# Moving layernorm statistics, weight sums and gates within one attention kernel, and Silu in place of Sigmoid and a product

## The chip, the cores and the metric

The kernel runs on one core of a Trainium2 chip. TensorE (PE) multiplies matrices into PSUM banks; VectorE (DVE), ScalarE (ACT) and GpSimd (POOL) work elementwise; SyncE (SP) mostly issues DMAs, which POOL and ACT can issue too. Each engine works through a list of instructions in order and waits on semaphores. The metric is device time in microseconds (us), less is better.

## What is computed

The reference, for 4 batches of 512 rows and 1024 columns, all fp32:

```python
xn = layernorm(x)
# attention per batch, 16 heads of 64, rotary on q and k, causal
q, k, v = xn @ Wq, xn @ Wk, xn @ Wv
s = softmax(causal(rot(q) @ rot(k).T / 8)) @ v @ Wo
# gate, over all 2048 rows
r = softmax(xn @ gate_w.T)                     # 8 experts
h = (xn * (r @ in_scale)) @ sign(weight).T * (r @ out_scale) + bias
out = x + s * (h * sigmoid(h))
```

## The kernel before

**Projections and attention.** The work runs in 16 slots, four groups g of heads for each of four batches b; (3,2) below is b = 3, g = 2. In a slot, PE computes q, k and v of one group with products of matrix quarters (seven products instead of eight, `project_qk` L323 and `project_v` L403). Sums of quarters are made for that by DVE: `form_w` (L269) makes S1 to S4 of weights, `form_x` (L291) makes T1 to T4 of the transposed, normalised rows X. For the last batch T1 is written in place, over the quarter b12 of X. Rotary (L310) takes the finished c of q or k, makes four swapped copies on ScalarE (L316, L317), so eight for a pair of units, one DVE product (L318) and two POOL operations (L319, L320).

Between the projection's matmuls, the attention of the group before is woven in. A unit u is two heads. For a unit: `scores` (L505), `softmax` (L530: mask and maximum on DVE, Exp on ScalarE L548, scaling by 1/sum on POOL L558), `transpose_blocks` (L566: ten DVE transposes of 32x32 blocks L576, then 16 DMAs L586 that put the blocks in place) and `values` (L593: matmul pv L601, copy of v out of PSUM on ScalarE L610, store). The slot has 84 steps of projection matmuls, cut into 16 pieces; `attention_pieces` (L843) says at which piece which part is written, for two units and the rest of the group before:

```python
            2: lambda: v and transpose_blocks(v),
            3 if last else 4: values_and_scores(w, u0),
            4 if last else 6: lambda: softmax(u0, 2, 0),
            8 if last else 10: lambda: transpose_blocks(u0),
```

The order on PE is written out by hand: it is the program's order. On the other engines a scheduler places the instructions, except those held by `keep_in_program_order`. A ring of four PSUM banks serves the projections (pj), pv, part of the scores and the gate's products; the rest of the scores has two banks of its own. A PE product that needs the next bank waits until the last reader of that bank's earlier content is done.

**Layernorm of the next batch** runs in the slots g = 2 and g = 3 of the first three batches, one pair of tiles of 128 rows each: per tile two half statistics (L171), the aggregate and Sqrt (`deviation` L174, L179), then `normalize` (L182: reciprocal L186, product L187), later two PE transposes of half a tile (`transpose_x` L195, xtp L201) and a store of the normalised rows to xn_d. The slot loop (L887 to L947) starts tile t0 at the slot's start, and tile t0 + 1 at piece 7. Sqrt and Exp need different function tables on ScalarE; the compiler puts an ACT_TABLE_LOAD where the table changes.

**The turn.** After the last slot the attention of the last two units remains. Beside it the gate of pairs 0 and 1 is computed with plain matmuls (`ffn` L1000; a pair is two tiles of 128 rows), its results pass through `gate` (L1018: product on DVE L1021, bias on POOL L1022), and `sum_wo` (L988) makes four sums of quarters of Wo, in four chunks each, on DVE, the third on POOL (L996). The schedule stands at L1052 to L1087; `dense(gates, n, m)` issues n steps of the gate, and a chunk of a sum after each of the first m. `values(u0)` and `values(u1)` come last.

**Output projection.** For pairs q = 0 to 7, `project_out` (L1213) multiplies the attention rows (ap) by Wo in seven products (wo, L1235), with sums of ap by `form_a` (L1096), and adds x and the gate. The `silu` (L1026) of pairs 0 and 1 is written just before this loop; for q from 2 on it follows each gate. `sign_sum` (L1115) makes four sums of sign matrices that the gates from pair 2 on need. `ahead` (L1335 on) lists what is written between the products of `project_out`, one entry at each of its stops (its yields).

Of the kernel before, what the change touches and what calls it, by code (L numbers as in the profile page):

```python
# [9 lines left out]
F32 = mybir.dt.float32  # L10
F32R = mybir.dt.float32r
AF = mybir.ActivationFunctionType
# [11 lines left out]
P = 128  # L24
# [18 lines left out]
def attn_gated_ffn_kernel(  # L43
# [138 lines left out]
    def normalize(b, t):  # L182
        xt = xin[b, t]
        mv, std = MV[b, t]
        rstd = st.tile([P, 1], F32, tag="rstd", name=f"rstd_{b}_{t}")
        nc.vector.reciprocal(rstd, std)  # L186
        nc.vector.tensor_scalar(xt, xt, mv[:, 0:1], rstd, op0=ALU.subtract, op1=ALU.mult)  # L187

    def layernorm(b, t):
        half_statistics(b, t, 0)  # L190
        half_statistics(b, t, 1)
        deviation(b, t)
        normalize(b, t)

    def transpose_x(b, t, g):  # L195
        if b not in X:
# [94 lines left out]
    def form_x(b, n):  # L291
        b11, b12, b21, b22 = quarters_x(b)
        if n > 1:
            f = fp.tile([P, 4, TH], F32, tag=f"T{n}", name=f"T{n}_{b}")
        elif b < B - 1:

            f = sgp.tile([P, 4, TH], F32, tag="last", name=f"T1_{b}")
        else:

            f = b12  # L300
        TF[b, n] = f
        x0, x1 = {
            1: lambda: (b12, b11),
            2: lambda: (b22, TF[b, 1]),
            3: lambda: (b22, b12),
            4: lambda: (b21, TF[b, 2]),
        }[n]()
        nc.vector.tensor_tensor(f, x0, x1, op=ALU.subtract)
# [534 lines left out]
    def attention_pieces(k, late):  # L843

        units = [(*groups[k], i) for i in range(2)]
        w, v = late
        u0, u1 = units

        def values_and_scores(before, u):
            def both():  # L850
                if before:
                    values(before)
                scores(u)
                softmax(u, 1, 3)

            return both

        pieces = [[] for _ in range(16)]  # L860

        last = k == len(groups) - 2
        plan = {
            2: lambda: v and transpose_blocks(v),
            3 if last else 4: values_and_scores(w, u0),
            4 if last else 6: lambda: softmax(u0, 2, 0),
            8 if last else 10: lambda: transpose_blocks(u0),
            9 if last else 12: values_and_scores(v, u1),
            10 if last else 14: lambda: softmax(u1, 2, 0),
        }  # L870
        if last:
            plan[14] = lambda: transpose_blocks(u1, ordered=True)
        for n, piece in plan.items():
            pieces[n].append(piece)
        return pieces, units
# [11 lines left out]
    for k, (b, g) in enumerate(groups):  # L887
        pieces = [[] for _ in range(9)]
        if k > 0:
            pieces, late = attention_pieces(k - 1, late)  # L890

        def at(n, piece):
            pieces[n].append(piece)


        if g == 0:
            routing = [lambda n=n: router(b, n) for n in range(3)]
            if k == 0:
                at(0, routing[0])
                at(1, lambda: (load_scales(in_scale), load_scales(out_scale)))  # L900
                at(2, routing[1])
                at(4, routing[2])
                at(5, lambda: split_scales(isc))
            else:
                if b < B - 1:
                    at(5, routing[0])
                at(8, routing[1])
                at(15, routing[2])
        elif g == 1 and b + 1 < B:

            at(11, lambda: [load_x(b + 1, t) for t in range(2)])
            if b == 0:
                at(1, lambda: split_scales(osc))
        elif g > 1 and b + 1 < B:
            t0 = 2 * (g - 2)
            layernorm(b + 1, t0)
            at(7, lambda: layernorm(b + 1, t0 + 1))
            for n, t, h in ((8, t0, 0), (9, t0, 1), (13, t0 + 1, 0), (14, t0 + 1, 1)):
                at(n, lambda t=t, h=h: transpose_x(b + 1, t, h))
            if g == 2:  # L920
                at(11, lambda: load_x(b + 1, 2))
                at(15, lambda: load_x(b + 1, 3))
        if k in (5, 9, 12, 14):
            n = {5: 0, 9: 2, 12: 4, 14: 6}[k]
            at(0, lambda: (load_sign(n), load_sign(n + 1)))
            at(8, lambda: make_sign(n))
            at(15, lambda: make_sign(n + 1))
        if b == B - 1:

            if g < 2:  # L930
                load_xn(g)
            if g in (1, 2):
                at(1, lambda: in_scales(g - 1, score_banks))
            if g == 3:
                z_place[0] = [xip.tile([P, E], F32, tag="x", name=f"z0_{i}") for i in range(2)]
                at(1, lambda: out_scales(0, score_banks))
        if k == 11:

            at(15, lambda: router(b + 1, 0))
        interleave(pieces, fill, 3 * 7 * 4 if k else 3 * 7 * 4 - 8)  # L940
        if g == NGRP - 1:
            for _ in fill:
                pass
            if b + 1 < B:
                for n in (3, 1, 2, 4):
                    form_x(b + 1, n)
                fill = projections(b + 1)  # L947
    pctx.close()
# [39 lines left out]
    def sum_wo(n, c):  # L988
        out_, x0, x1 = {
            1: (t1, b12, b11),  # L990
            2: (t2, b22, t1),
            3: (t3, b22, b12),
            4: (t4, b21, t2),
        }[n]
        engine = nc.gpsimd if n == 3 else nc.vector
        difference = engine.tensor_tensor(out_[:, c, :], x0[:, c, :], x1[:, c, :], op=ALU.subtract)  # L996
        if n != 3:
            tc.keep_in_program_order(difference)

    def ffn(q, i, k):  # L1000

# [23 lines left out]

    def silu(q, i, k):  # L1026
        z = Z[q, i][:, k * HALF : (k + 1) * HALF]
        g = work.tile([P, HALF], F32, tag="g", name=f"g_{q}_{i}_{k}")
        nc.scalar.activation(g, z, AF.Sigmoid)
        nc.gpsimd.tensor_tensor(z, z, g, op=ALU.mult)  # L1030

    def gated(q):
        for i in range(2):
# [13 lines left out]

    u0, u1 = units = [(*groups[-1], i) for i in range(2)]
    w, v = late
    sums = iter([(n, c) for n in (1, 3, 2, 4) for c in range(4)])  # L1050

    def dense(gates, n, n_sums=0):  # L1052
        for i in range(n):
            next(gates)
            if i < n_sums:
                sum_wo(*next(sums))
# [7 lines left out]
    dense(gates, 8)  # L1064

    split(1, 0)
    transpose_blocks(u0, ordered=True)
    load_wo(1)
    values(v)
    scores(u1)  # L1070
# [7 lines left out]
    out_scales(1, score_banks)  # L1078
    dense(gates, 2)
    transpose_blocks(u1, (nc.sync, nc.scalar), ordered=True)  # L1080
    dense(gates, 10, 10)
    values(u0)
    dense(gates, 2, 2)
    values(u1)
    for _ in gates:
        pass
# [28 lines left out]
    def sign_sum(n):  # L1115

        if n == 3:
            TS[n] = [sg[4], sg[5]]
        else:
            t = (app if n == 4 else tsp).tile(  # L1120
                [P, 2, E], F32R, tag="ap" if n == 4 else f"T{n}", name=f"Tsg{n}"
            )
            TS[n] = [t[:, r, :] for r in range(2)]
        for r in range(2):
            x0, x1 = {
                1: lambda: (sg[4 + r], sg[r]),
                2: lambda: (sg[6 + r], TS[1][r]),
                3: lambda: (sg[6 + r], sg[4 + r]),
                4: lambda: (sg[2 + r], TS[2][r]),
            }[n]()  # L1130
            nc.vector.tensor_tensor(
                TS[n][r], x0.bitcast(F32), x1.bitcast(F32), op=ALU.subtract
            )

    PARTS = {}
# [185 lines left out]
            )  # L1321

    load_xn(2)

    for q in range(2):
        for i in range(2):
            for k in range(2):
                silu(q, i, k)
    for q in range(len(pairs)):
        if q < 2:  # L1330
            for n in range(1, 5):
                form_a(q, n)
        if q == 0:
            load_at(1)
        ahead, later = [], []  # L1335
        if q == 0:
            ahead = [lambda n=n: sign_sum(n) for n in (1, 2, 3)]
        elif q < len(pairs) - 1:
            ahead = [
                lambda: None,  # L1340
                lambda: (in_scales(q + 1), later.append(first_parts(q + 1))),
                lambda: out_scales(q + 1),
                lambda: later.pop()(),
            ]
        for _ in project_out(q):
            if ahead:
                ahead.pop(0)()
        if q != 1 and q + 1 < len(pairs):
            load_at(max(q + 1, 2))
        if q == 1:  # L1350
            sign_sum(4)
        if 1 <= q < len(pairs) - 1:
            gated_by_strassen(q + 1)
            if q + 2 < len(pairs):
                load_xn(q + 2)
# [58 lines left out]
```

## Time and profile before

| | us |
|---|---|
| median of 3 runs (lowest to highest) | 1114.5 (1114.41 to 1115.24) |
| profiled execution | 1114.49 |
| its span | 1112.6 |
| PE busy | 1086.9 |
| DVE, POOL, ACT busy | 896.9, 575.5, 469.9 |
| POOL multiplies of silu (L1030), 32 of them | 47.6 |
| ACT_TABLE_LOAD for Sqrt (L179) and Exp (L548), 12 each | 15.4 and 15.4 |
| first PE instruction, end of the last | 1.5, 1108.1 |

The slots end and the turn begins near 785 us; the loop over pairs begins near 824 us and takes the rest. The mean clock granted to PE is 0.998 of full speed.

How to read it: the first part of the page gives busy time, share of the span and number of instructions of each engine. A group of instructions is named by its line, engine, and what it writes and reads (`p<-sc,nmx` writes p from sc and nmx). A row of the waits says which engine and line waited, after the arrow for what, then the total in us, how often, and the longest. A row of a timeline gives the start, the time from the first start to the last end of the instructions in it, their number, and in brackets how long the engine was idle before and what ended that. Instructions that follow one another overlap by about 0.1 us. A stretch's granted clock comes from a table by windows.

### The profile page before, as it was taken

The page shows a single profiled execution, that of the slowest core. Times are in us where ns is not written, and L with a number is a line of the kernel's source. Part 1 is how long each engine was busy: PE and PEld are TensorE (multiplying, and loading weights), DVE is VectorE, ACT ScalarE, POOL GpSimd, SP SyncE. Part 2 cuts the span into 40 slices and gives each one's busy share as a digit, 9 for nine tenths or more (in the row PEclk, how much of TensorE's full clock was granted, in tenths as well). Part 3 has the DMA queues.
Part 4 walks back from the last instruction along what each step waited for, and adds up shares of the span by engine and source line. Part 5 has one row for each costly group of instructions (what it writes and reads, how often), then busy time and mean ns, then how long its engine had stood idle before and what let it go on. Part 6 is the DMA issues. An engine that isn't in the chain of part 4 may idle for free.

```text
span 1112.6 us, 15955 instructions
## 1 busy us (share of the span) xinstructions
PE 1086.9 (98%) x5176; PEld 788.0 (71%) x5176; DVE 896.9 (81%) x1736; ACT 469.9 (42%) x1080; POOL 575.5 (52%) x594
## 2 busy tenths in 40 slices
PE   9999999999989999998999999999979999999998
PEld 8887677787768778776877787777744545655664
DVE  7887989788897978889787987887797777667764
ACT  2553665454366545436653452664520222122220
POOL 0672555555255555525552662674585455444535
PEclk9999999999999999999999999999999999999999
DMA  9415556644655664465566544554683222431431
GB/s 322 144 60 149 174 148 159 194 136 120 178 168 155 169 177 135 120 180 168 159 169 195 171 149 141 151 131 127 165 252 114 81 91 103 156 118 47 142 114 57
DMA packets 86898, 163.88 MB, mean 147 GB/s; under 512 B 13472, under 2 KB 49056, under 8 KB 80800
## 3 DMA queue, kind: packets, MB, share of 16 engines
q1 hardware_dynamic: 80528, 152.91, 46.2%
q0 software_dynamic: 4576, 8.39, 2.2%
q10 hardware_dynamic: 1712, 1.57, 0.5%
q8 instruction: 41, 0.67, 0.3%
q14 instruction: 41, 0.34, 0.1%
HBM read 95.45 MB, written 25.43 MB: 109 GB/s over the span
## 4 chain that ended last, share of the span: by engine, by line
PE 74%; DVE 11%; POOL 4%; issue 3%; ACT 3%; DMA 2%; SPq 1%; POOLq 0%; DVEq 0%; ACTq 0%
PE pj L335 25%; PE wo L1235 16%; PE pj L422 13%; PE ff L1175 7%; PE sc L522 5%; PE pv L601 5%; POOL p L558 2%; DVE y L576 2%; DVE S L289 2%; DVE nmx L545 1%; SPq L586 1%; PE xtp L201 1%; DVE w L289 1%; DMA xn_d<-X 1%; ACT sw L317 1%
## 5 line engine op out<-in xcount | busy, mean ns | idle before, releaser
L558 POOL TENSOR_SCALAR p<-p,rs 128x256 f32<-128x256 f32 (+3 forms) x256 | 181.8, 726 | 189.0 <-DVE rs L556 144.3
L548 ACT ACTIVATE p<-sc,nmx 128x256 f32<-128x256 f32 (+3 forms) x256 | 132.8, 529 | 92.9 <-DVE nmx L545 72.6
L319 POOL TENSOR_TENSOR sw<-sw,sin_sb 128x512 f32<-128x512 f32 x64 | 89.6, 1400 | 94.4 <-ACT sw L317 93.0
L335 PE MATMUL pj<-X,w 128*128 128x256 f32 x576 | 134.4, 382 | 0.2 <-ACT X L207 0.2
L335 PE MATMUL pj<-T,S 128*128 128x256 f32 x512 | 118.2, 381 | 8.5 <-ACT v L610 7.2
L335 PEld LDWEIGHTS pj<-X,w 128*128 128x128 f32 x576 | 108.1, 190 | 18.6 <-issue 2.9
L576 DVE STREAM_TRANSPOSE y<-p 128x256 f32<-128x256 f32 x320 | 110.2, 408 | 12.7 <-POOL p L558 12.7
L316 ACT ACTIVATE sw<-c 32x512 f32<-32x512 f32 x128 | 80.3, 628 | 81.0 <-DVE c L349 79.3
L335 PEld LDWEIGHTS pj<-T,S 128*128 128x128 f32 x512 | 96.0, 190 | 23.6 <-ACT v L610 8.8
L335 PE MATMUL pj<-T,w 128*128 128x256 f32 x448 | 107.2, 382 | 0.0
L545 DVE TENSOR_REDUCE nmx<-sc 128x1 f32<-128x256 f32 (+3 forms) x160 | 104.9, 683 | 1.3
L320 POOL TENSOR_TENSOR rot<-rot,sw 128x512 f32<-128x512 f32 x64 | 94.1, 1470 | 5.0
L335 PEld LDWEIGHTS pj<-T,w 128*128 128x128 f32 x448 | 83.3, 190 | 15.2 <-issue 4.6
L422 PE MATMUL pj<-w,X 128*128 128x256 f32 x416 | 93.8, 380 | 0.0
L422 PEld LDWEIGHTS pj<-w,X 128*128 128x128 f32 x416 | 78.7, 190 | 11.0 <-issue 0.5
L542 DVE TENSOR_TENSOR sc<-sc,mask 128x256 f32<-128x256 f32 (+1 forms) x160 | 57.2, 371 | 30.8 <-PE sc L522 30.8
L317 ACT ACTIVATE sw<-c 32x512 f32<-32x512 f32 x128 | 80.4, 628 | 1.7
L522 PE MATMUL sc<-rot,rot 64*128 64x128 f32 (+3 forms) x512 | 80.3, 444 | 0.4 <-DVE v L448 0.3
L422 PE MATMUL pj<-w,T 128*128 128x256 f32 x352 | 80.2, 381 | 0.0
L610 ACT COPY v<-pv 128x512 f32<-128x512 f32 x32 | 18.6, 581 | 145.6 <-PE pv L601 132.7
L385 POOL TENSOR_TENSOR part<-part,part 128x256 f32<-128x256 f32 x32 | 25.9, 809 | 102.1 <-ACT part L384 81.8
L601 PE MATMUL pv<-p,v 128*64 128x256 f32 (+3 forms) x512 | 76.0, 439 | 2.7 <-DVE xp L996 2.7
(177 smaller groups left out, 2042.9 us busy)
## 6 DMA issues: line engine op xcount, KB each, us to landing
p<-y SPq DMA_DIRECT2D x504, 80.0 KB, 2.1
w<-in_wqk SPq DMA_DIRECT2D x31, 1024.0 KB, 5.3
w<-in_wv SPq DMA_DIRECT2D x16, 1024.0 KB, 5.2
x<-in_x SPq DMA_DIRECT2D x16, 512.0 KB, 3.5
at_d<-v SPq DMA_DIRECT2D x32, 256.0 KB, 2.7
xp<-xn_d SPq DMA_DIRECT2D x16, 512.0 KB, 4.5
ap<-at_d SPq DMA_DIRECT2D x16, 512.0 KB, 5.0
xr<-in_x SPq DMA_DIRECT2D x32, 256.0 KB, 3.0
```

The source lines that it names most:

```text
L317: nc.scalar.activation(sw[r + 32 : r + 64, :], c[r : r + 32, :], AF.Copy, scale=sc)
L319: nc.gpsimd.tensor_tensor(sw, sw, sin_sb, op=ALU.mult)
L320: nc.gpsimd.tensor_tensor(rot, rot, sw, op=ALU.add)
L335: nc.tensor.matmul(ps, lhsT=wq[:, k, :], rhs=xq[:, k, :], start=(k == 0), stop=(k == 3))
L422: nc.tensor.matmul(ps[:, j, :], lhsT=xq[:, k, j * P : (j + 1) * P], rhs=wq[:, k, :], start=(k == 0), stop=(k == 3),)
L522: nc.tensor.matmul(head(i, h), lhsT=Q[u][r : r + D, i * P : (i + 1) * P], rhs=K[u][r : r + D, : (i + 1) * P], start=True, stop=True,)
L545: nc.vector.tensor_reduce(nmx[:, hs], v, AX.X, ALU.max, negate=True)
L548: nc.scalar.activation(pt[:, h, :], ps[h], AF.Exp, bias=nmx[:, h : h + 1], accum_out=ssum[:, h : h + 1],)
L558: nc.gpsimd.tensor_scalar(pt[:, h, :], pt[:, h, :], rs[:, h : h + 1], 1.0, op0=ALU.mult, op1=ALU.mult,)
L576: nc.vector.transpose(out[:, :, :, o : o + 32], src.rearrange("p h (b c) -> p h b c", b=4))
L601: nc.tensor.matmul(by_block[r : r + D, :, 32 * j :], lhsT=V[u][:, j, r : r + D], rhs=PT[u][:, :, o : o + 32 * (TPB - j)], start=(j == 0), ...
L1235: nc.tensor.matmul(ps, lhsT=lhs[:, k, :], rhs=rhs[:, k, :], start=(first and k == 0), stop=(k == 3), skip_group_check=not first,)
```

## The change

1. In the six layernorm slots the statistics of both tiles are written at the slot's start, followed by the normalize of t0; that of t0 + 1 comes at piece 3. The PE transposes of t0 move from pieces 8 and 9 to 7 and 8.
2. `transpose_blocks(u0)` is written at piece 9 instead of 10, except in the last slot.
3. For the last batch, T2 is T3 + b11 instead of b22 - T1 (the same value), and the order is 3, 2, 4, 1.
4. `silu` is one Silu on ScalarE, in place, without the POOL product. For pairs 0 and 1 it is written inside the first `project_out`, at its second and fourth stop.
5. All weight sums are on VectorE and in program order: 1 and 2 before the loop over pairs, 3 after the third sum of `form_a(0, ...)`, 4 at the second stop of the first `project_out`.
6. The sign sums are held in program order and are spread over the first two pairs.
7. The DMAs of `transpose_blocks(u0)` in the turn are issued by SP and POOL in turn instead of SP alone.

```diff
--- before.py
+++ after.py
@@ -186,11 +186,10 @@
         nc.vector.reciprocal(rstd, std)
         nc.vector.tensor_scalar(xt, xt, mv[:, 0:1], rstd, op0=ALU.subtract, op1=ALU.mult)
 
-    def layernorm(b, t):
+    def layernorm_scales(b, t):
         half_statistics(b, t, 0)
         half_statistics(b, t, 1)
         deviation(b, t)
-        normalize(b, t)
 
     def transpose_x(b, t, g):
         if b not in X:
@@ -299,6 +298,10 @@
 
             f = b12
         TF[b, n] = f
+        if b == B - 1 and n == 2:
+
+            nc.vector.tensor_tensor(f, TF[b, 3], b11, op=ALU.add)
+            return
         x0, x1 = {
             1: lambda: (b12, b11),
             2: lambda: (b22, TF[b, 1]),
@@ -864,7 +867,7 @@
             2: lambda: v and transpose_blocks(v),
             3 if last else 4: values_and_scores(w, u0),
             4 if last else 6: lambda: softmax(u0, 2, 0),
-            8 if last else 10: lambda: transpose_blocks(u0),
+            8 if last else 9: lambda: transpose_blocks(u0),
             9 if last else 12: values_and_scores(v, u1),
             10 if last else 14: lambda: softmax(u1, 2, 0),
         }
@@ -913,9 +916,12 @@
                 at(1, lambda: split_scales(osc))
         elif g > 1 and b + 1 < B:
             t0 = 2 * (g - 2)
-            layernorm(b + 1, t0)
-            at(7, lambda: layernorm(b + 1, t0 + 1))
-            for n, t, h in ((8, t0, 0), (9, t0, 1), (13, t0 + 1, 0), (14, t0 + 1, 1)):
+
+            layernorm_scales(b + 1, t0)
+            layernorm_scales(b + 1, t0 + 1)
+            normalize(b + 1, t0)
+            at(3, lambda: normalize(b + 1, t0 + 1))
+            for n, t, h in ((7, t0, 0), (8, t0, 1), (13, t0 + 1, 0), (14, t0 + 1, 1)):
                 at(n, lambda t=t, h=h: transpose_x(b + 1, t, h))
             if g == 2:
                 at(11, lambda: load_x(b + 1, 2))
@@ -942,7 +948,7 @@
             for _ in fill:
                 pass
             if b + 1 < B:
-                for n in (3, 1, 2, 4):
+                for n in (3, 1, 2, 4) if b + 1 < B - 1 else (3, 2, 4, 1):
                     form_x(b + 1, n)
                 fill = projections(b + 1)
     pctx.close()
@@ -992,10 +998,9 @@
             3: (t3, b22, b12),
             4: (t4, b21, t2),
         }[n]
-        engine = nc.gpsimd if n == 3 else nc.vector
-        difference = engine.tensor_tensor(out_[:, c, :], x0[:, c, :], x1[:, c, :], op=ALU.subtract)
-        if n != 3:
-            tc.keep_in_program_order(difference)
+        tc.keep_in_program_order(
+            nc.vector.tensor_tensor(out_[:, c, :], x0[:, c, :], x1[:, c, :], op=ALU.subtract)
+        )
 
     def ffn(q, i, k):
 
@@ -1025,9 +1030,7 @@
 
     def silu(q, i, k):
         z = Z[q, i][:, k * HALF : (k + 1) * HALF]
-        g = work.tile([P, HALF], F32, tag="g", name=f"g_{q}_{i}_{k}")
-        nc.scalar.activation(g, z, AF.Sigmoid)
-        nc.gpsimd.tensor_tensor(z, z, g, op=ALU.mult)
+        nc.scalar.activation(z, z, AF.Silu)
 
     def gated(q):
         for i in range(2):
@@ -1047,7 +1050,7 @@
 
     u0, u1 = units = [(*groups[-1], i) for i in range(2)]
     w, v = late
-    sums = iter([(n, c) for n in (1, 3, 2, 4) for c in range(4)])
+    sums = iter([(n, c) for n in (1, 2, 3, 4) for c in range(4)])
 
     def dense(gates, n, n_sums=0):
         for i in range(n):
@@ -1064,7 +1067,7 @@
     dense(gates, 8)
 
     split(1, 0)
-    transpose_blocks(u0, ordered=True)
+    transpose_blocks(u0, (nc.sync, nc.gpsimd), ordered=True)
     load_wo(1)
     values(v)
     scores(u1)
@@ -1078,9 +1081,9 @@
     out_scales(1, score_banks)
     dense(gates, 2)
     transpose_blocks(u1, (nc.sync, nc.scalar), ordered=True)
-    dense(gates, 10, 10)
+    dense(gates, 10, 4)
     values(u0)
-    dense(gates, 2, 2)
+    dense(gates, 2)
     values(u1)
     for _ in gates:
         pass
@@ -1128,8 +1131,10 @@
                 3: lambda: (sg[6 + r], sg[4 + r]),
                 4: lambda: (sg[2 + r], TS[2][r]),
             }[n]()
-            nc.vector.tensor_tensor(
-                TS[n][r], x0.bitcast(F32), x1.bitcast(F32), op=ALU.subtract
+            tc.keep_in_program_order(
+                nc.vector.tensor_tensor(
+                    TS[n][r], x0.bitcast(F32), x1.bitcast(F32), op=ALU.subtract
+                )
             )
 
     PARTS = {}
@@ -1321,26 +1326,34 @@
             )
 
     load_xn(2)
-
-    for q in range(2):
-        for i in range(2):
-            for k in range(2):
-                silu(q, i, k)
+    def silu_pair(q):
+
+        for i, k in ((0, 0), (1, 1), (1, 0), (0, 1)):
+            silu(q, i, k)
+
     for q in range(len(pairs)):
         if q < 2:
             for n in range(1, 5):
                 form_a(q, n)
+                if q == 0 and n == 3:
+                    for c in range(4):
+                        sum_wo(3, c)
         if q == 0:
             load_at(1)
         ahead, later = [], []
         if q == 0:
-            ahead = [lambda n=n: sign_sum(n) for n in (1, 2, 3)]
+            ahead = [
+                lambda: None,
+                lambda: (silu_pair(0), [sum_wo(4, c) for c in range(4)]),
+                lambda: sign_sum(1),
+                lambda: silu_pair(1),
+            ]
         elif q < len(pairs) - 1:
             ahead = [
-                lambda: None,
+                lambda: q == 1 and sign_sum(2),
                 lambda: (in_scales(q + 1), later.append(first_parts(q + 1))),
                 lambda: out_scales(q + 1),
-                lambda: later.pop()(),
+                lambda: (later.pop()(), q == 1 and sign_sum(3)),
             ]
         for _ in project_out(q):
             if ahead:
```

## The prediction, on record before the change was run

> **What bounds the kernel now.** I read the page first. TensorE (PE) is busy for 1086.9 of 1112.6 us, and PE carries 74% of the chain that ended last. So a microsecond on another engine counts only where PE waits for it. The waits of PE alone say where:
>
> ```profile
> PE 1086.9 (98%) x5176; PEld 788.0 (71%) x5176; DVE 896.9 (81%) x1736; ACT 469.9 (42%) x1080; POOL 575.5 (52%) x594
> PE pj L335 <- ACT v L610: 7.2, 4, 1.9
> PE xtp L201 <- ACT p L548: 4.2, 3, 1.4
> PE wo L1235 <- ACT g L1029: 3.0, 1, 3.0
> PE pv L601 <- DVE xp L996: 2.7, 1, 2.7
> PE pj L335 <- DVE T L308: 1.3, 1, 1.3
> PE os L780 <- ACT p L548: 0.3, 1, 0.3
> ```
>
> In each row (us in total, times, longest) the name after the arrow is the work that ended last. Outside the start and the end, PE has some 19 us to lose, and these rows are nearly all of it. From 845 us on, where pair after pair runs at one beat, the PE timeline has no gap. So the trace's windows that matter are six places: three slots with layernorm (139, 334, 528 us, alike), 592 us, 628 us, and the turn from attention to projection (784 to 836 us).
>
> The second view is the timeline of ScalarE (ACT) in the first layernorm slot:
>
> ```profile
> 132.05 0.63 ACT L316 ACTIVATE sw<-c 32x512 f32<-32x512 f32 x1 [6.65 <-DVE c L349]
> 135.16 0.56 ACT L610 COPY v<-pv 128x512 f32<-128x512 f32 x1
> 135.74 0.63 ACT L317 ACTIVATE sw<-c 32x512 f32<-32x512 f32 x1
> ...
> 137.66 1.28 ACT L548 ACT_TABLE_LOAD   x1
> 138.96 0.47 ACT L548 ACTIVATE p<-sc,nmx 128x256 f32<-128x256 f32 x1
> ```
>
> Eight rotary copies (L316/317) wait for DVE's c. The copy of v, which frees the bank of pv for PE's next product, stands behind five of them, and PE waits 1.79 us for it (135.77). The Exp stands behind all eight and a table load; PE waits 1.38 us for it (139.58). Both waits start at the late c.
>
> The third view is PE in the turn:
>
> ```profile
> 822.09 2.37 PE L601 MATMUL pv<-p,v 128*64 128x512 f32 x16 [2.68 <-DVE xp L996]
> 824.39 3.70 PE L1235 MATMUL wo<-wo,ap 128*128 128x512 f32 x8
> 831.12 5.37 PE L1235 MATMUL wo<-xp,S 128*128 128x512 f32 x8 [3.03 <-ACT g L1029]
> ```
>
> Of the two eight-record products the second took 5.2 us (831.12 to 836.32) instead of 3.43. The granted clock was 0.56 from 831.1 to 834.0 and 0.82 to 836.4. The two waits cost 2.68 + 3.03, and the clock 1.77 more.
>
> **The change, part by part.** Where a price depends on order, I use the order of instructions that each engine's program has after the change; it is static and holds no times.
>
> *Layernorm in three slots.* Statistics of both tiles move to the start, so the second half of the slot loses two statistics (1.27 us a pair), the aggregate and a normalize (1.03), 2.65 us of DVE with the rest. Each Sqrt between Exps costs two table loads of 1.28; six slots go from four to two, 12 fewer. At the slot's start the added DVE work lies beside PE work: its S3 waits for a weight that lands at 120.66, and PE's first wait comes 15 us later. If that cover were gone, 2.65 us would show. The c of the second half should come about 2 us earlier (130.0 instead of 132.05). But in ScalarE's new order v is behind all eight copies, not five. Eight copies (0.64 each) and v end at 130.0 + 5.1 + 0.6 = 135.7, as before (135.72). So the first stall stays; the second, with its table load gone, should go: 3 × −1.4 = **−4.2**. Bounds: −4.7, and −1 if c gains only a little. Slots g = 3 have no PE wait: 0, unless the one-piece-earlier transposes (x at pieces 7 and 8, p at 9) delay something.
>
> *Transposes of p at piece 9, and v behind more copies, in slots without layernorm.* In slots (1,0) and (2,0) v moves from behind five copies to behind eight. The row near 230 us: copies start at 230.39, v ends at 234.06, PE takes the bank at 234.47 with no wait. With c 0.45 earlier, v ends near 235.65: a new stall of about 1.3, twice: **+2.6** (1.6 to 4.6). In slot (3,0) DVE's transposes now wait for POOL's p (L558, 614.4 against 612.95), c is 0.9 later and v one copy (0.64) further back: **+1.5** (0.7 to 2.1) on the 1.86 already there. In (3,2) DVE waits likewise (712.2), c moves to 717.6, v ends at 723.4 where PE wants it at 721.1: **+2.3** (1.5 to 2.8).
>
> *Last batch's T2.* It is made as T3 + b11 instead of b22 − T1, and is second in line. T1 is written in place, so it waits until the store of xn_d has landed:
>
> ```profile
> 589.96 1.23 DVE L308 TENSOR_TENSOR X<-X 128x1024 f32<-128x1024 f32 x1 [6.91 <-DMA xn_d<-X]
> 592.48 1.23 DVE L308 TENSOR_TENSOR T<-X,T 128x1024 f32<-128x1024 f32 x1
> ```
>
> T2 and T4 no longer stand behind it; DVE had been idle for 6.91 us. The stall of 1.26 at 592.50 goes: **−1.3** (0 if T1 is next to be late).
>
> *Silu in one function.* Sixteen Sigmoid halves and 32 POOL multiplies (47.6 us in all, 1.46 to 1.53 each) become Silu in place. In the beat after 845 us no PE wait hangs on them: 0. There the hiding work is PE's own; removing POOL work can't speed it. Whether a Silu takes longer than a Sigmoid (0.63) the trace doesn't show; up to 1.3 would still fit, ScalarE being busy for 53 of 230 us there.
>
> *The turn.* Taken away: POOL's sum (5.43 us) and eight multiplies (15.5), moved in part to DVE (4 × 0.68). With POOL active, DVE's sums took 1.0 to 1.75 and one 4.74 instead of 0.68, so DVE gains more than it gets. The Trainium skill's "GPSIMD Engine Reference" (4.1 Engine selection) advises VectorE for tile add and multiply and calls GpSimd about twice as slow with two inputs; the rows say 1.27–1.38 against 0.68. Added: the Silus of pairs 0 and 1. They are written later, but the scheduler has put two of them early, between the Exps of the last two softmaxes, each with a load there and a load back. What a load costs decides here:
>
> ```profile
> 825.10 1.28 ACT L1029 ACT_TABLE_LOAD   x1
> 826.40 1.15 ACT L1029 ACTIVATE g<-z 128x512 f32<-128x512 f32 x2
> ```
>
> The next function starts 1.30 after the load. The skill's "ScalarE: Activation LUTs" (What ACT_TABLE_LOAD costs) adds a drain of 1.38, 2.66 us per switch. By the page, two switches would put 5.3 + 0.6 us before the Exp; by the row 2.6 + 0.6, less its idle 1.08 before: 2.1 later (789.7 for 787.57). I take the row. The u0 transposes come 1 us later; the Exps of u1, whose load inherits their wait, end 1.45 later (os stall 0.35 to 1.8: **+1.5**). POOL now issues eight of the p loads too (about 0.55 each), ahead of u1's scaling, which had slack of 6.45, and is done by 808.2 as before. DVE's transposes of u1 end 1.1 later and PE's pv (822.09) is 1.0 later, **+1.0**. By then DVE has sums 1 and 2 and then S2 without POOL beside it: ready near 824.5, against 831 now. So the wait of 3.03 goes, pv's delay is left, and PE's product starts at about 828.85 instead of 831.12. As the two idles no longer follow one another, I expect the clock to stay up: −1.77. The skill's "TensorE: Matmul & The Clock Gate" (Part 1) puts the drop at an idle window of 3.4 us. Neither idle reached that, yet the clock fell after 2.68 and 3.03 within 12 us, so the row allows that pv's wait alone (some 3.7) drops it again: by the page the slow clock stays, by the nearest rows (single waits up to 1.9, clock 1.00) it goes. Net of the turn, 828.85 − 831.12 − 1.77 = **−4.0**, which contains the two plus terms; range −5 to +1.5.
>
> **Sum.** −4.2 + 2.6 + 1.5 + 2.3 − 1.3 − 4.0 = −3.1. The profiled execution took 1114.49 for a span of 1112.6, and the median is 1114.5, so both sums start at the same point: **1111.4 us**, −0.28%.
>
> **Rivals.**
> 1. *The copies of v don't hurt.* If c gains more than 2 us, or the bank's wait is covered by another bank of the ring, the +6.4 vanish: 1105. For it: four banks. Against: today's v waits hit this very place.
> 2. *Slower: the copy of v behind all eight copies.* One mechanism in up to eight slots: three more copies are 1.9 us. If c does not come earlier in the layernorm slots (because DVE's queue refills with the moved transposes), their first stall grows by 1.9 − 0.7 each instead of shrinking: +3.6 in place of −4.2, hence −3.1 + 7.8 = +4.7 with the turn as forecast: 1119; with half of it, 1116. It decides as soon as c gains less than about 1 us. Against: 2.65 us of DVE work does leave that stretch.
> 3. *No change.* The stalls move to another row, as in the first stall above, and the turn's Silus eat its gain: within 2 us of 1114.5. The change doesn't do what it says in one point: gates "later" are early in ScalarE's program.
>
> **Chances.** A measurement of this kernel tells about 0.2% (2.2 us) from no change. My forecast (1109 to 1113) 0.40, rival 1 (below 1109) 0.14, no change 0.22, rival 2 (above 1116.7) 0.24. The forecast's upper edge lies within the 0.2%. So faster 0.49, same 0.21, slower 0.30. The range, 1107 to 1117, takes in the bounds of the turn and half of each rival.
>
> **What would show it.** Right: no wait of xtp on Exp in the slots at 139, 334, 528 us; none at 592; PE waits on v (L613 after the change) in (1,0), (2,0), (3,0), (3,2) of 1.2 to 3.5 us; 19 table loads; the wo product after 828 us at clock 1.00. Wrong: v waits missing at 234 us (rival 1) or three times above 2.5 us in layernorm slots (rival 2); a second slow-clock stretch in the turn; or waits of PE in the beat after 845 us, which would mean that Silu is dearer than I took it.

## The result, and the profile after

| | before | after |
|---|---|---|
| median of 5 runs, us (lowest to highest) | 1115.24 (1114.41 to 1117.05) | 1110.42 (1109.2 to 1111.51) |
| ratio, 95% interval | | 0.9952 (0.9939 to 0.9965) |
| profiled execution / its span | 1114.49 / 1112.6 | 1110.42 / 1108.7 |
| end of the last PE instruction | 1108.07 | 1103.03 |
| POOL busy | 575.5 | 518.9 |

The change saves 4.8 us by the medians; the forecast was 1111.4, a saving of 3.1. The waits of PE after the change (total, times, longest):

```profile
PE pj L338 <- ACT v L613: 8.5, 7, 2.3
PE os L783 <- ACT p L551: 2.0, 1, 2.0
...
PE pj L338 <- ACT p L551: 1.5, 2, 1.1
PE pj L425 <- ACT p L551: 0.5, 1, 0.5
PE pv L604 <- issue: 0.4, 1, 0.4
```

The rows of xtp on Exp (4.2), of wo on the gate (3.0), of pv (2.7) and of T (1.3) are gone. The row of v has grown from four waits to seven, os (the product with the output scales, r @ out_scale) waits 2.0 instead of 0.3, and Exp appears as a cause at new places. So the kernel took out some 11 us of waits and let in about 5 us.

ScalarE in the first layernorm slot:

```profile
129.78 0.63 ACT L319 ACTIVATE sw<-c 32x512 f32<-32x512 f32 x1 [4.02 <-DVE c L352]
...
134.92 0.59 ACT L613 COPY v<-pv 128x512 f32<-128x512 f32 x1
135.53 0.47 ACT L551 ACTIVATE p<-sc,nmx 128x256 f32<-128x256 f32 x1
```

By the traces' own times the copies start 2.3 us sooner (132.05 before). PE itself runs 0.60 later here in this execution, so against PE they start 2.9 sooner. No table load stands before Exp, and v is behind all eight copies. PE's wait on v is 1.20 us here (1.79 before).

PE in the turn:

```profile
822.58 2.38 PE L604 MATMUL pv<-p,v 128*64 128x512 f32 x16 [0.36 <-issue]
824.88 3.70 PE L1240 MATMUL wo<-wo,ap 128*128 128x512 f32 x8
828.42 3.60 PE L1240 MATMUL wo<-xp,S 128*128 128x512 f32 x8
831.85 3.60 PE L1240 MATMUL wo<-wo,ap 128*128 128x512 f32 x8
```

No bracket stands at 828.42: the wait of 3.03 is gone, and the product takes its 3.43 us, at full clock. But the granted clock now falls earlier, behind the wait on v in slot (3,0) and behind the wait of os. A row gives the window, its length, PE busy, granted clock, DMA share and GB/s:

```profile
624.00:626.00 2.00, 2.00 (x7) 0.60 0.51 115
626.00:628.00 2.00, 2.00 (x7) 0.55 0.46 104
...
804.00:806.00 2.00, 1.35 (x5) 0.83 0.88 313
806.00:808.00 2.00, 2.00 (x6) 0.50 0.99 293
808.00:810.00 2.00, 2.00 (x9) 0.82 0.96 356
```

For a sum that misses nothing I subtract the start of the same PE instruction in two traces, at the borders of the stages. What a stage adds to that difference is what it gained or lost, in waits and in clock:

| stage (us against before) | forecast | after | what the waits say |
|---|---|---|---|
| layernorm slots, three pairs | -4.2 | -3.67 | v 1.20, 1.38, 1.39 for 3 x 1.79; xtp 3 x 1.38 gone; Exp 0.37, 1.12, 0.48, 0.14, 0.14 new |
| slots (1,0) and (2,0) | +2.6 | +0.92 | v 0.18 each |
| last batch's T2 (592 us) | -1.3 | -1.73 | 1.26 gone |
| slot (3,0) | +1.5 | +1.33 | v 2.34 for 1.86; the clock fell |
| slot (3,2) | +2.3 | +2.08 | v 1.81 |
| turn, up to 845 us | -4.0 | -4.01 | os 2.01 for 0.35, pv 0.36 for 2.68, 3.03 gone; the clock fell behind os, not behind 3.03 |
| pairs from 845 us on | 0 | -0.57 | no row shows it, see below |
| sum | -3.1 | -5.65 | |

The stages begin 0.6 us later in this execution, and from the last matmul to the end of the span it takes 1.1 us longer (5.66 against 4.56), which leaves 3.9 us of span.

A wait costs more than its row says, by about 0.27 us: the wait of 0.18 in slot (1,0) cost 0.44, that of 1.81 in (3,2) cost 2.08, and one of 1.77 with the layernorm order alone cost 2.04. A matmul there takes 0.38 us and the next starts 0.21 us after it, and a bracket does not count the overlap that is lost. At the start of slot (2,2) it is 0.7 us, for which no row gives a reason.

The table compares one execution of each kernel; of 55 others of the kernel before, timed beside the experiments, the eight with a mean granted clock of 1.000 took 1111.4 to 1112.6 us, and the twenty at 0.992 or less took 1114.2 to 1117.3.

### The profile page after: what moved, and what is told of

It is laid out like the page before. It is cut to its first block, busy times and chain, and to the rows that moved or that the text cites. A ratio compares the mean times of both kernels' runs of the same rounds, so it can differ in the third digit from the quotient of the medians.

```text
span 1108.7 us, 15895 instructions
## 1 busy us (share of the span) xinstructions
PE 1087.4 (98%) x5176; PEld 790.2 (71%) x5176; DVE 870.4 (79%) x1740; ACT 461.3 (42%) x1072; POOL 518.9 (47%) x566
## 5 line engine op out<-in xcount | busy, mean ns | idle before, releaser
L338 PE MATMUL pj<-T,S 128*128 128x256 f32 x512 | 120.5, 385 | 8.5 <-ACT v L613 8.5
L322 POOL TENSOR_TENSOR sw<-sw,sin_sb 128x512 f32<-128x512 f32 x64 | 85.1, 1330 | 81.1 <-ACT sw L320 75.4
L323 POOL TENSOR_TENSOR rot<-rot,sw 128x512 f32<-128x512 f32 x64 | 90.8, 1419 | 5.0
```

Source lines behind the costliest of these rows:

```text
L322: nc.gpsimd.tensor_tensor(sw, sw, sin_sb, op=ALU.mult)
L323: nc.gpsimd.tensor_tensor(rot, rot, sw, op=ALU.add)
L338: nc.tensor.matmul(ps, lhsT=wq[:, k, :], rhs=xq[:, k, :], start=(k == 0), stop=(k == 3))
```

## The experiments

Each kernel ran on a chip beside the kernel before; the ratios are to that.

**Layernorm order alone.** Edit of the kernel before: part 1 of the change.

> The kernel before with the layernorm order alone (part 1 of the change); all else as before. My theory, from the two traces: in the three slots g = 2 the wait of xtp on Exp (1.38 each) goes and the wait on v falls from 1.79 to 1.2 to 1.4, while DVE's added work at the slot's start makes the first Exp of the slot late for PE by 0 to 1.1 us: about -3 us against before, no new wait of more than 0.5 in slots g = 3. Rival (the fewer table loads alone matter): -4.2 and no wait on Exp at the slots' starts. Rival (nothing; the whole gain is elsewhere): within 1 us of before, the stalls move to the row of v.

Measured: 1105.18, ratio 0.992 (0.9898 to 0.9943), some 9 us for the expected 3. In the slots g = 2 no wait on v and none of xtp is left. (The profiled execution, at 1108.65, was the slowest of four.) ScalarE there:

```profile
129.01 0.63 ACT L315 ACTIVATE sw<-c 32x512 f32<-32x512 f32 x1 [4.49 <-DVE c L348]
...
132.12 0.56 ACT L609 COPY v<-pv 128x512 f32<-128x512 f32 x1
132.70 0.63 ACT L316 ACTIVATE sw<-c 32x512 f32<-32x512 f32 x1
```

v is still behind five copies, ends at 132.68, and PE wants its bank at 133.94. The layernorm slots gain 6.95 us (3.67 with the whole change), and the wait at 592 us shrinks from 1.26 to 0.45. At the starts of slots new waits on Exp came: 0.31 and 1.17 in slots g = 2, as expected, and 1.77 and twice 0.25 in slots g = 3, where 0.5 at most was expected. PE now reaches these places sooner, and DVE's maxima, for which Exp waits, do not come sooner by as much. Both rivals fall, and so does my own picture that the layernorm order puts v behind eight copies. The edit also moves two transposes one piece earlier; the two were not taken apart.

**Silu alone.** Edit of the kernel before:

```diff
-        nc.scalar.activation(g, z, AF.Sigmoid)
-        nc.gpsimd.tensor_tensor(z, z, g, op=ALU.mult)
+        nc.scalar.activation(z, z, AF.Silu)
```

> The kernel before with Silu in place of Sigmoid and the POOL product, nothing moved. Theory that the turn's gain comes from taking POOL's products away from beside DVE's sums: the wait of 3.03 before the second wo product falls below 1.2 us, no slow clock behind it, and the whole is 2 to 4 us below before, although two Silus come early between the Exps and the wait of os grows to 2.0. Rival, that the gain comes from moving the weight sums behind the first products: the wait of 3.03 stays over 2.5, and with the early Silus the time is at or up to 1.5 us above before.

Measured: 1117.13, ratio 1.0026 (1.0017 to 1.0036): slower. Its waits of PE:

```profile
PE pj L335 <- ACT v L610: 7.2, 4, 1.9
PE os L780 <- ACT p L548: 4.2, 1, 4.2
PE pv L601 <- DVE z_t L996: 2.4, 1, 2.4
```

Half of the theory holds: without POOL's products the wait of 3.03 is gone. But the early Silus make os wait 4.17 us, the clock falls to 0.50 for some 6 us, and the turn costs 1.40 more; the pairs after 845 us give 0.92 of that back. The clock also fell behind the waits on v at 137, 331, 526 and 629 us, where in the trace of before the same waits left it at 1.00. In slot (3,0) that cost 1.47; in the three slots g = 2 only 0.1 each, because PE, being slower, no longer met the wait of xtp (1.38).

**Silus held.** Edit of the changed kernel:

```diff
-        nc.scalar.activation(z, z, AF.Silu)
+        gated = nc.scalar.activation(z, z, AF.Silu)
+        if q < 2:
+            tc.keep_in_program_order(gated)
```

> The changed kernel with the eight Silus of pairs 0 and 1 held in program order on ScalarE, so behind the last Exps; four table loads fewer. Theory that the early Silus cost what the wait of os and the slow clock behind it show (2.01 us and about 1.4 more): os waits 0.4 us, no slow clock at 806 us, and the time is 1 to 2.5 us below the changed kernel. Rival: PE only waits later, for the blocks of p of the last unit (pv near 822 us), and the time is within 0.5 us of the changed kernel.

Measured: 1110.2, ratio 0.9966 (0.995 to 0.9981); no gain over the change, so the rival holds. os waits 0.35, and pv 2.65 instead of 0.36, with a slow clock of its own (0.50 at 820 us). The blocks of p of the last unit land no earlier, so it is the same whether PE waits for os or for pv. The program of the slots is that of the changed kernel, yet the wait on Exp at 500 us is 0.30 here and 1.12 there; one trace sizes such a wait only roughly.

**v on VectorE.** Edit of the changed kernel, for the second unit, up to slot (3,1):

```diff
-        nc.scalar.copy(
+        copy = nc.vector.tensor_copy if i == 1 and (b, g) < (3, 2) else nc.scalar.copy
+        copy(
```

> The changed kernel with the copy of v of the second unit on VectorE instead of ScalarE, in the slots up to (3,1), so that it stands behind no rotary copies. Theory that these copies hold PE's bank: all seven waits on v go (8.5 us), and with them the slow clock at 624 us (about 1): 6 to 9 us below the changed kernel (1101 to 1104). Rival, that PE only runs on to the next late result (Exp of the same unit, c of the same slot): waits of about the same sum on Exp, and 0 to 3 us below the changed kernel. Slower, if DVE's added 0.7 us in front of the maxima delays Exp and the scores' banks: up to 3 us above it.

Measured: 1101.07, ratio 0.9879 (0.9862 to 0.9897), 0.73% below the changed kernel by the ratios, about 8 us. The waits of PE:

```profile
PE pj L425 <- ACT p L551: 2.3, 3, 1.8
...
PE pj L338 <- ACT p L551: 1.8, 2, 0.9
...
PE pj L338 <- DVE v L614: 1.0, 1, 1.0
```

Of seven waits on v one of 1.04 is left, and the clock stays up at 617 us. So the theory holds for the larger part, and the rival for a part: Exp's rows grow from 2.0 to 4.1.

**Transposes back at piece 10.** Edit of the changed kernel: part 2 undone.

> The changed kernel with the transposes of u0 back at piece 10, everything else as changed. ScalarE's order then has v behind five copies again in the slots where the change put it behind eight. Theory that the move to piece 9 causes the waits on v in the changed kernel (1.2 and twice 1.4 in the slots g = 2, 0.2 twice, 1.8 in (3,2), and part of the 2.3 in (3,0)): only one wait on v is left (1.9 in (3,0)), and the time is 4 to 6.5 us below the changed kernel (about 1105). Rival, that the layernorm order itself puts v late: the waits in the slots g = 2 stay and the time is within 1.5 us of the changed kernel.

Measured: 1102.89, ratio 0.9905 (0.9882 to 0.9927). The waits of PE:

```profile
PE pj L425 <- ACT p L551: 2.2, 3, 1.7
PE os L783 <- ACT p L551: 2.0, 1, 2.0
PE pj L338 <- ACT v L613: 1.9, 1, 1.9
```

v waits once, in (3,0), as expected; it is behind five copies again in the other places, and the layernorm slots gain 7.8 us instead of 3.67. So within the changed kernel piece 9 costs 0.47% by the ratios, about 5 us; the traces' stages add to 8.4.

**Sigmoid kept.** Edit of the changed kernel: part 4's function undone, all moves kept.

> The changed kernel with Sigmoid and the POOL product kept in place of Silu; all moves of sums, gates and transposes as changed. No gate function comes between the last Exps, since the product's buffer g does not exist before then. Theory that the moves, not the function, bring the turn's gain: os waits 0.4, no wait before the second wo product, and the time is within 1 us of the changed kernel with the Silus held (1110.2). Rival, that POOL's products beside DVE's sums are what made the sums late: a wait of 1.5 to 3 before the second wo product and 2 to 4 us above.

Measured: 1111.13, ratio 0.9968 (0.9955 to 0.998). No wait before the second wo product; pv waits 2.71. Up to 845 us the turn gains 3.4 us here and 3.3 with the Silus held: the moves bring all of it, and the function nothing. In the pairs after that Silu is worth 1.5 us more: here they lose 1.07 to before, with the Silus held they gain 0.48. Half of it is a wait at 885 us, 0.92 against 0.18. Within the intervals the two times are the same. Which of the moves does it (sums, sign sums, gates or queues) was not taken apart.

**Queues in the turn.** Edit of the changed kernel: piece 10, Silus held, u0 on SP alone, u1 on three queues.

```diff
-                move = queues[a % len(queues)].dma_start(
+                move = queues[(4 * n + a) % len(queues)].dma_start(
...
-    transpose_blocks(u0, (nc.sync, nc.gpsimd), ordered=True)
+    transpose_blocks(u0, ordered=True)
...
-    transpose_blocks(u1, (nc.sync, nc.scalar), ordered=True)
+    transpose_blocks(u1, (nc.sync, nc.scalar, nc.gpsimd), ordered=True)
```

> The changed kernel with the transposes at piece 10, the Silus of pairs 0 and 1 held behind the last Exps, and in the turn the DMAs of p for u0 on SP alone (as before the change) and for u1 spread over SP, ACT and POOL (five or six each in place of eight). With the Silus held PE waited 2.65 us for p of u1 (pv at 819 us) and ran at half clock for 2.4 us after it. Theory: POOL's scaling of u1 is no longer behind its eight DMA issues, and the last issue comes 1.8 us sooner, so that wait falls below 1 us, no slow clock follows, and the time is 2.5 to 4 us below the changed kernel with piece 10 alone. Rival: DVE, not the queues, ends last there (transposes of u1 behind a sum and a split): the wait stays above 2 and the time is within 1 us of piece 10 alone.

Measured: 1102.99, ratio 0.9903 (0.9883 to 0.9923): no gain over piece 10 alone. The wait for pv is 4.45, longer. SP's issues of u1 in this kernel, and what SP waited for from 803 to 815 us:

```profile
805.46 8.12 SPq L589 DMA_DIRECT2D p<-y  x6
SPq L589 <- DMA p<-y: 3.3, 1, 3.3
SPq L589 <- DMA wo<-in_wo: 1.3, 1, 1.3
```

Six issues took 8.1 us, where eight took 4.96 with the Silus held. The issues themselves were not slower: SP stood 4.6 us for earlier transfers to land, among them loads of Wo (L977). With u0 on SP alone its 16 issues take 10.0 us, and these loads are issued behind them, until 6 us before DVE was done with u1 (11 us before with the Silus held). The last landed at 809.7, when most of u1 had been issued. So the experiment mixed two edits, and the one to u0 probably spoiled the other; u1 on three queues alone was not run.

**The same with v on VectorE.** 

> The same with the copy of v of the second unit on VectorE up to slot (3,1). Theory: with the transposes at piece 10 only the wait of 1.9 in (3,0) is left on v, it falls to about 1.0 and may keep the clock up (1.4 more): 0.5 to 2.5 us below the kernel with v on ScalarE. Rival: the added DVE work delays the maxima, PE waits on Exp instead, and it is 0 to 2 us above.

Measured: 1104.86, ratio 0.9916 (0.9899 to 0.9933). The wait in (3,0) fell to 1.08, but PE waited for Exp 1.12 us at 354 and 547 us instead of 0.24: the rival. On VectorE the copy helps only where v would come late otherwise.

**Piece 9 alone.** Edit of the kernel before:

```diff
-            8 if last else 10: lambda: transpose_blocks(u0),
+            8 if last else 9: lambda: transpose_blocks(u0),
```

> The kernel before with the transposes of u0 at piece 9 instead of 10, nothing else. ScalarE's order has v behind seven or eight rotary copies in the slots g = 2, and behind eight in three others, instead of five. Theory that this part alone costs time: the first wait in the slots g = 2 grows from 1.8 to 2.5 or more, new waits on v of 0.2 (twice) and 1.8 appear, that of (3,0) grows by 0.5; 2 to 5 us above before. Rival, that earlier transposes bring c forward by as much as the copies push v back: within 1 us of before.

Measured: 1108.36, ratio 0.9942 (0.9927 to 0.9957): faster. My theory falls, and the rival too. The waits of PE:

```profile
PE pj L335 <- ACT v L610: 9.1, 7, 2.3
PE pv L601 <- DVE xp L996: 2.7, 1, 2.7
```

The new waits on v came as expected (0.18 twice, 1.79, and 2.33 in (3,0)). But in the slots g = 2 the earlier c takes xtp's wait from 1.38 to 0.10 and v's from 1.79 to 1.55: 1.7 to 1.75 gained per pair of slots, 5.2 in all. The wait at 592 us went too (1.2). And the turn gained 2.6 with nothing changed in it, since the wait of 3.03 was not there. DVE's sums S for the second wo product, and POOL's products of silu, in before and then here:

```profile
825.88 3.42 DVE L1106 TENSOR_TENSOR S<-ap 128x512 f32<-128x512 f32 x2
829.23 1.75 DVE L1106 TENSOR_TENSOR S<-S,ap 128x512 f32<-128x512 f32 x1
827.17 7.13 POOL L1030 TENSOR_TENSOR z<-z,g 128x512 f32<-128x512 f32 x4
823.32 2.35 DVE L1106 TENSOR_TENSOR S<-ap 128x512 f32<-128x512 f32 x2
825.60 0.68 DVE L1106 TENSOR_TENSOR S<-S,ap 128x512 f32<-128x512 f32 x1
825.98 7.52 POOL L1030 TENSOR_TENSOR z<-z,g 128x512 f32<-128x512 f32 x4 [1.46 <-ACT g L1029]
```

In before the last S ends at 830.98 and PE starts at 831.12. The product reads S, and not the g of the Sigmoid that the row of the waits names, so S is what it waited for. Here DVE is 2.56 us ahead of before, but POOL's products only 1.19: behind the wait of 2.69 for pv the clock fell, pv and the copy of v ended later, and with them the Sigmoids that stand behind that copy on ScalarE. So S was formed almost without POOL beside it and was done at 826.28, before PE came at 827.02.

**T2 alone.** Edit of the kernel before: part 3.

> The kernel before with T2 of the last batch as T3 + b11 and the order 3, 2, 4, 1, nothing else. Theory: the wait of 1.26 at 592 us goes and nothing is late in its place, 1.3 to 1.7 us below before (about what three rounds can tell). Rival: T1, now last, is late by as much, and the wait stays.

Measured: 1113.88, ratio 0.9988 (0.9978 to 0.9998). The wait at 592 us is gone with nothing late in its place, and that stage gains 1.53. In this execution the wait of 1.86 in (3,0) dropped the clock, and gave 1.71 back.

**Piece 10, one v on VectorE.** Edit of the changed kernel: piece 10, and the copy of v on VectorE for the unit (2,2,1) alone.

> The changed kernel with the transposes at piece 10, and the copy of v on VectorE only for the unit whose copy falls into slot (3,0), where PE still waits 1.86 us for it. Theory: that wait falls to about 1.0 as it did with all these copies on VectorE, nothing else moves, and the time is 0.8 to 2 us below piece 10 alone (1102.9). Rival: VectorE's next maxima come 0.7 later and the gain is lost: within 0.5 us.

Measured: 1102.39, ratio 0.9891 (0.9872 to 0.991). The wait in (3,0) fell to 1.07 and the stage gained 0.78; against piece 10 alone the intervals overlap, so the step is seen in the trace and not in the time.

**Silus held, v on VectorE.** Edit of the changed kernel: the two edits of these names together.

> The changed kernel, transposes at piece 9 as changed, with the Silus of pairs 0 and 1 held behind the last Exps and v of the second unit on VectorE up to slot (3,1). v on VectorE alone gave 1101.1. Theory, from the Silus held alone (the wait of os and its slow clock were replaced by a wait of 2.65 before pv and its slow clock): within 1 us of 1101.1, and within 2 us of piece 10 with v of one unit on VectorE. Rival: the Silus' loads cost time after all, once the slots end sooner: 1.5 us or more below 1101.1.

Measured: 1101.68, ratio 0.9883 (0.9863 to 0.9903): as v on VectorE alone. os waits 0.37 instead of 1.98, pv 3.37 instead of 0.43, as in the pair of kernels above, and no slow clock follows it. The best kernels here are 1.2% below before, and the change itself 0.5%.

## Why the prediction was right, and where not

*Layernorm slots.* Right in sum (-3.67 for -4.2) and in the main mechanism: Exp's wait went with its table load, and c came sooner. On before's clock (PE was 0.60 behind) c came 2.9 us sooner for 2 forecast, and v ended at 134.9 for 135.7, so the first wait shrank by 0.4 to 0.6 instead of staying. The cover at the slot's start was taken as whole, but of the slots g = 2 it held in the first batch only: 0.37 and 1.12 show later, and 0.48 and twice 0.14 in slots g = 3. The step that failed is the cause given for v behind eight copies. It was listed under the layernorm order; with the layernorm order alone v stands behind five, with piece 10 restored too, and with piece 9 alone behind seven, so the transposes at piece 9 put it there. The number of rival 1 (1105, the +6.4 gone) belongs beside piece 10 (1102.89), where v is back behind five copies; that the layernorm order alone took 1105.18 is a coincidence, as it lacks the gain of the turn.

*Slots (1,0), (2,0).* Right in kind, the term mis-sized: +0.92 for +2.6. The forecast took c to come 0.45 us sooner. The copies started at 227.76, and PE itself is 1.26 ahead there, so on before's clock at 229.02 against 230.39: 1.4 sooner. The wait is 0.18 instead of 1.3.

*Slots (3,0), (3,2).* +1.33 and +2.08 for +1.5 and +2.3. In (3,2) the mechanism is right: the copies start at 717.4 on before's clock (c at 717.6 forecast), and v ends at 723.1 (723.4). In (3,0) the number is luck. The forecast had c 0.9 us later; the copies start 0.9 sooner on before's clock (623.66 against 624.53), and the scores before the wait gain 0.83 by it. Then PE stands 0.48 longer for v, and the slow clock behind that costs 1.69, which was not in the sum. The kernels with piece 10 have none of the three.

*T2.* The wait of 1.26 went, nothing took its place. It gives 1.53, alone and in the change: the wait and the 0.27 that its row does not count. The other 0.20 of the table's 1.73 comes at the end of slot (2,3), as it does in the other slots g = 3 and with the layernorm order alone; no row says from what.

*Turn.* On before's clock (PE was 0.46 ahead) pv started at 823.04 (823.1 forecast), the product at 828.88 (828.85), at full clock. os waited 2.01 (1.8 forecast). What the forecast lacked is the slow clock behind os, about 1.6 us; it cost nothing, since PE would have stood before pv anyway, where 0.36 of 2.68 is left. With one v on VectorE and piece 10 the clock stayed up behind os, pv waited 2.00 instead, and the turn gained the same 4.0. The early Silus, a plus term of 1.5 in the working, cost nothing for the same reason (Silus held). With Silu alone, where os waited 4.17, the turn lost 1.40.

*Silu in the beat.* Forecast as 0, and here a term was missing. With Silu alone PE gains 0.92 on before from 845 us on, and with the whole change 0.57. It comes in like steps of 0.16 us, once in each pair, at the same two products (ff, L1175): before starts them 0.32 us after their predecessors, the kernels with Silu 0.23, as their neighbours. The kernel with the Sigmoid kept has no such steps. "No PE wait hangs on them" was read from rows that leave out waits under 0.15 us; what held these products is in no row, and stays open. The change loses 0.23 again at the first pair, with a new wait of 0.15 (886 us). A Silu takes 0.63 us, no longer than a Sigmoid. (The working counts sixteen Sigmoid halves; there are 32.)

*What ends last in the turn.* The forecast laid the old wait of 3.03 to DVE's sums beside POOL, and the traces bear it out. In before three sums of Wo on DVE took 7.04 us beside POOL's own sum; after, the same three took 1.85:

```profile
814.52 1.85 DVE L1002 TENSOR_TENSOR xp<-wo,xp 128x512 f32<-128x512 f32 x3
```

And the last S before the product took 1.75 us beside POOL's products, and 0.68 without them. Three different edits removed the wait: taking POOL's products away (Silu alone), moving sums and gates (Sigmoid kept), and piece 9, by way of a slow clock. In all three POOL's products no longer lie beside S. So the wait's disappearance does not say which edit is needed; what the three share does.

*Sum.* The direction and most of the terms are right; that the total lies within 1 us of the measurement is in part luck, as (3,0) shows, and as executions of the kernel before alone spread over some 6 us. Of the signs it named, the 19 table loads, the missing waits of xtp and at 592 us, and the wo product at clock 1.00 came; waits on v of 1.2 or more in (1,0) and (2,0) did not. The parts do not add. Alone, the layernorm order gives 0.8%, piece 9 gives 0.6%, T2 0.1%, Silu costs 0.3%; the whole change, with its 4 us in the turn, gives 0.5%. Layernorm order and piece 9 both bring c forward, and PE's wait can be taken out only once. With both, c does not come sooner still (copies at 129.78, against 129.01 with the first alone), and ScalarE's order puts v behind three more copies. That is shown by piece 10 restored; why the scheduler orders them so stays open.

## What to carry to other kernels

Look at the order of an in-order engine after a change, not only at what comes sooner: work that frees a PSUM bank can slip behind work that became ready earlier. Two edits that relieve the same wait must be tried apart and together; in the layernorm slots each alone gained more (6.95 and 5.2 us) than the change with both (3.67). Before a stall is priced, ask what PE would wait for next: in the turn, os and pv shared one end time, so moving a wait from one to the other was worth nothing. And a list of waits has a least length: compare the starts of the same instructions in two traces, and what the list leaves out shows.

## What the runs showed of the hardware that I had not expected

The clock fell behind single waits well below the 2.68 and 3.03 that I took for a pair: in slot (3,0) the same wait of 1.86 us left it at 1.00 in before and with piece 10 restored, and brought it to 0.50 for about 3.4 us with the layernorm order alone, Silu alone and T2 alone, at a price of 1.5 to 1.7 us. The wait of 2.33 did it in after and with piece 9 alone, and not with the Silus held. In the fourteen traces no PE wait of 1.0 to 1.77 us behind the start was followed by a slow clock, 18 of the 42 waits from 1.79 to 3.37 were, and the longest of these, 3.37 (Silus held, v on VectorE), was not. The Trainium skill's "TensorE: Matmul & The Clock Gate" (Part 1) says that the window of about 3.4 us runs free of the kernel, which fits that equal waits differ, and puts the drop at one idle window; the measurement decides here, and it says that an idle of little more than half of that can be enough. So a wait of 1.8 us or more costs its length, or up to 1.7 us more, and no trace here tells beforehand which. The spread of the kernel before with its clock fits that.
